# A two-layer convolution kernel: the prologue put in another order, the statistics' matrix product moved behind a group, small copies moved to ScalarE

## The chip, the cores and the metric

The kernel runs on 1 core of one Trainium2 chip. The metric is the device time of one execution in microseconds; lower is better. The engines are named as in the profile: PE (TensorE matmul), PEld (its weight loads), DVE (VectorE), ACT (ScalarE), POOL (GpSimd), SP (the queue that issues most DMAs).

## What is computed

Two layers, one after the other, on x of shape (8, 32, 252, 252), fp32. Each normalises its input over groups of two channels (16 groups, mean and variance over 2 x 252 x 252 values), convolves it with a 5 x 5 kernel over reflected padding (32 channels to 32), and adds the layer's input:

```python
def _gn(v, G=16, eps=1e-5):
    B_, C_, H_, W_ = v.shape
    g = v.reshape(B_, G, C_ // G, H_, W_)
    m = jnp.mean(g, axis=(2, 3, 4), keepdims=True)
    s = jnp.var(g, axis=(2, 3, 4), keepdims=True)
    return ((g - m) / jnp.sqrt(s + eps)).reshape(v.shape)

x = x + _L0_conv_ref(_gn(x), L0_conv_weight)   # _L0_conv_ref: reflect pad by 2, 5x5 convolution (written with fft2)
x = x + _L1_conv_ref(_gn(x), L1_conv_weight)
```

## The kernel before, in words

**Layout.** An image is split by parity of row and column into four quarter images (polyphase). The 128 partitions hold 4 parities x 32 channels; in each a padded quarter image has 128 x 128 points. A 5 x 5 convolution of the image becomes, on these 128 planes, a 3 x 3 convolution with 128 x 128 matrices. Along the rows it is done by a short transform (six products `m0` to `m5` give four output rows); along the columns by three accumulating matmuls with shifted views.

**Groups.** A *step* (b, l, T) is one group of 16 rows of image b in layer l. There are NG = 8 groups to an image and layer; a run of 8 is a *phase*. The phases are (0,0), (1,0), (0,1), (2,0), (1,1), ... , (7,1): 16 phases, 128 steps, 15 phase boundaries. Each step has six products of three fp32 matmuls, and the profile shows each matmul as two records, so 36 records.

**One step, in the order in which the code emits it.** Each engine works through its own instructions in that order (`manual_schedule`).
- `fetch` of step i+3 (SP: image rows into a buffer of two halves), chunk loads for the statistics (SP), `variance` in the step before a boundary.
- `transform` of step i+1 (DVE, L317 to L333): from the padded group `g` to the six inputs `v`.
- `scales` in the step before a boundary (DVE, L280 to L285: reciprocal standard deviation and `mr`).
- `conv` of step i: PE makes the products in the order m1, m2, m3, m4, m0, m5 (L359). ACT copies m1 (L374, adding the offset) and m3 (L382) out of PSUM, DVE combines (L378 to L396) into the output `y`. Between the products stand three hooks:
  - `after_1`: `prepare` of step i+2: layer 0 takes two ACT copies (L131) and three small POOL copies of the padding columns (L132, L134); layer 1 loads g from a DRAM scratch.
  - `after_3`: before a boundary `scale_matrices` (ACT, L292: the phase's matrices u = raw matrices x reciprocal deviation); for the group before, `to_output` (ACT copies L437, DMA) in layer 1 or `output_sums` (ACT, L251 and L252) in layer 0; `input_sums` of a chunk (ACT, L243 and L244).
  - `after_4`: `averages` two steps before a boundary, and `find_offset` and `add_own` one step before.
- At the end of a layer-0 `conv`, `to_scratch`: three small POOL copies of padding columns (L408 to L410) and the DMAs to the scratch (L418).

**Statistics.** Sums and sums of squares go by chunk into a slot tile. `averages` (L256 to L260) adds the slots on DVE (`tot`, L257) and multiplies them on PE with a membership matrix into PSUM (`pm`, L259). `variance` (L265 to L270) copies `pm` to SBUF (`me`) and takes the root on ACT; `scales` makes `mr`; `find_offset` (L304, L306) multiplies the matrix `total` with `mr` on PE (`po`) and copies it on DVE (`off`), which L374 adds; `add_own` (L300, DVE) adds the layer's own input to u. Of the three matmuls of a product, the first needs no result of `add_own`.

**Weights.** `load_taps` clears a tile on POOL (L143) and fills it with 8 DMAs on ACT's queue (L151). `make_matrices` takes sums (L162, L165) and makes six rows per tap on DVE (L171 to L180), clears u on POOL (L182) and copies the rows into it on ACT (L190, 8 copies). `make_own` makes a constant on POOL (L204, 24 operations).

**Prologue.** Taps of layer 0, rows of step 0, then the 8 chunks of image 0 through three buffers (a chunk's sum on DVE L241, its squares on ACT L244, in place, then the next load into that buffer), with the rest in between. The second layer's taps are loaded and turned into matrices behind step 1.

**Buffers.** Seven PSUM buffers for products, one for pm and po; two each for g, v and y.

Of the kernel before, what the change touches and what calls it, by code (L numbers as in the profile page):

```python
# [37 lines left out]
F32 = mybir.dt.float32  # L38
BF16 = mybir.dt.bfloat16
AF = mybir.ActivationFunctionType  # L40
ALU = mybir.AluOpType
AX = mybir.AxisListType

P = 128
# [12 lines left out]
def tile_conv_preact_x2(ctx: ExitStack, tc: tile.TileContext, x: bass.AP, w0: bass.AP, w1: bass.AP, out: bass.AP):  # L57
# [60 lines left out]
    def prepare(b: int, l: int, T: int):  # L118

        nr = min(GR + 2, PB - GR * T)  # L120
        g = gpool.tile([P, GR + 2, PB], F32, tag="g", name=f"g_{b}_{l}_{T}")
        gt[b, l, T] = g
        if nr < GR + 2:
            nc.gpsimd.memset(g[:, nr:, :], 0.0)  # L124
        if l:
            nc.sync.dma_start(g[:, :nr, :], scratch[b][:, GR * T : GR * T + nr, :])
            return
        t = xt.pop((b, T))
        h0, h1 = halves
        for pc in range(2):  # L130
            nc.scalar.copy(g[halves[pc], :nr, 1 - pc : 1 - pc + NB], t[:, :nr, 1 - pc : W : 2])  # L131
        nc.gpsimd.tensor_copy(g[h0, :nr, 0 : PB : PB - 1], g[h0, :nr, 1 : NB : NB - 2])  # L132
        for dst, src in ((126, 125), (127, 1)):
            nc.gpsimd.tensor_copy(g[h1, :nr, dst : dst + 1], g[h1, :nr, src : src + 1])  # L134


    ident = const.tile([P, P], F32, tag="ident", name="ident")
# [1 line left out]

    def load_taps(l: int, w: bass.AP):  # L140

        t = prep.tile([P, 2, 3, K, C], F32, tag="taps", name=f"taps{l}")
        nc.gpsimd.memset(t, 0.0)  # L143
        for pc in range(2):
            for pr in range(2):
                for rp in range(2):
                    d = pr - rp
                    rows = [a for a in range(3) if 0 <= 2 * a - d < K]
                    lo, n = rows[0], len(rows)
                    first = 2 * lo - d  # L150
                    nc.scalar.dma_start(  # L151
                        t[quad(pc, pr), rp, lo : lo + n], w[:, first : first + 2 * n - 1 : 2, :, :]
                    )
        return t

    def make_matrices(l: int, t: bass.AP):
        r = prep.tile([P, NF, 2, K, C], F32, tag="rows", name=f"rows{l}")
        s = prep.tile([P, 2, K, C], F32, tag="rsum", name=f"rsum{l}")
        v = nc.vector

        sums = prep.tile([P, C], F32, tag="sums", name=f"sums{l}")
        v.tensor_reduce(sums, t.rearrange("p r a k o -> p o (r a k)"), axis=AX.X, op=ALU.add)  # L162
        tot = const.tile([P, 4, C], F32, tag=f"total{l}", name=f"total{l}")
        for q in range(4):
            v.tensor_scalar(tot[:, q, :], sums, 0.25, None, ALU.mult)  # L165
        total.append(tot.rearrange("p q o -> p (q o)"))
        flat = lambda a: a.rearrange("p r k c -> p r (k c)")
        t0, t1, t2 = (flat(t[:, :, a]) for a in (2, 1, 0))
        s = flat(s)
        rf = [flat(r[:, f]) for f in range(NF)]  # L170
        v.tensor_scalar(rf[0], t0, 0.25, None, ALU.mult)  # L171
        v.tensor_copy(rf[5], t2)
        v.tensor_add(s, t0, t2)
        v.tensor_add(rf[1], s, t1)
        v.tensor_sub(rf[2], s, t1)
        v.tensor_scalar(r[:, 1:3].rearrange("p f r k c -> p (f r k c)"), r[:, 1:3].rearrange("p f r k c -> p (f r k c)"), -1.0 / 6, None, ALU.mult)
        v.scalar_tensor_tensor(s, t2, 4.0, t0, ALU.mult, ALU.add)
        v.scalar_tensor_tensor(rf[3], t1, 2.0, s, ALU.mult, ALU.add)
        v.scalar_tensor_tensor(rf[4], t1, -2.0, s, ALU.mult, ALU.add)
        v.tensor_scalar(r[:, 3:5].rearrange("p f r k c -> p (f r k c)"), r[:, 3:5].rearrange("p f r k c -> p (f r k c)"), 1.0 / 24, None, ALU.mult)  # L180
        u = const.tile([P, NF, 3, 2, 2, C], F32, tag=f"u{l}", name=f"u{l}")
        nc.gpsimd.memset(u, 0.0)  # L182
        for pc in range(2):
            for cp in range(2):
                d = pc - cp
                cols = [b for b in range(3) if 0 <= 2 * b - d < K]
                lo, n = cols[0], len(cols)
                first = 2 * lo - d
                for rp in range(2):
                    nc.scalar.copy(  # L190
                        u[halves[pc], :, lo : lo + n, 1 - cp, 1 - rp, :],
                        r[halves[pc], :, rp, first : first + 2 * n - 1 : 2, :],
                    )
        raw.append(u.rearrange("p f b c r o -> p (f b c r o)"))
# [17 lines left out]
    def make_averages():  # L212
        for l, pattern in enumerate(("p (q g e) -> p g q e", "p (g q e) -> p g q e")):
            kinds = {"q": 4, "e": 2}
            member = const.tile([P, C // 2], F32, tag=f"member{l}", name=f"member{l}")
            nc.vector.tensor_reduce(member, ident.rearrange(pattern, **kinds), axis=AX.XY, op=ALU.add)
            a = const.tile([P, 4, C // 2, 2], F32, tag=f"avg{l}", name=f"avg{l}")
            for q in range(4):
                for e in range(2):
                    nc.vector.tensor_scalar(a[:, q, :, e], member, 1.0 / COUNT, None, ALU.mult)  # L220
            avg.insert(0, a.rearrange("p q g e -> p (q g e)"))


# [22 lines left out]
    def output_sums(b: int, T: int, y: bass.AP):  # L246
# [4 lines left out]
        nc.scalar.activation(junk[:, :rows], view, AF.Identity, accum_out=st[:, 0, T : T + 1])  # L251
        nc.scalar.activation(junk[:, :rows], view, AF.Square, accum_out=st[:, 1, T : T + 1])  # L252

    def averages(b: int, l: int):

        tot = small.tile([P, 2], F32, tag="tot", name=f"tot_{b}_{l}")  # L256
        nc.vector.tensor_reduce(tot, sums.pop((b, l)), axis=AX.X, op=ALU.add)  # L257
        pm = ps_stat.tile([P, 2], F32, tag="pstat", name=f"pm_{b}_{l}")
        nc.tensor.matmul(pm, avg[l], tot, start=True, stop=True)  # L259
        norm[b, l] = pm  # L260

    def variance(b: int, l: int):
# [24 lines left out]

    ut, offset = {}, {}

    def scale_matrices(b: int, l: int):  # L290
        u = upool.tile([P, NF, 3, P], F32, tag="u", name=f"u_{b}_{l}")
        nc.scalar.activation(  # L292
            u.rearrange("p f b m -> p (f b m)"), raw[l], AF.Identity, scale=norm[b, l][:, 0:1]
        )
        ut[b, l] = u

    def add_own(b: int, l: int):
# [4 lines left out]
    def find_offset(b: int, l: int):  # L302
        po = ps_stat.tile([P, 1], F32, tag="pstat", name=f"po_{b}_{l}")
        nc.tensor.matmul(po, total[l], norm.pop((b, l))[:, 1:2], start=True, stop=True)  # L304
        offset[b, l] = small.tile([P, 1], F32, tag="off", name=f"off_{b}_{l}")
        nc.vector.tensor_copy(offset[b, l], po)  # L306


    vt = {}
# [37 lines left out]
    def conv(b: int, l: int, T: int, after_1, after_3, after_4):  # L347
# [46 lines left out]
        m5 = product(5)  # L394
        v.tensor_add(d1, m5, d1)  # L395
        v.scalar_tensor_tensor(yo[3], d2, 8.0, d1, ALU.mult, ALU.add)  # L396
        if l == 0:
            to_scratch(b, T, y)
        return y

    def to_scratch(b: int, T: int, y: bass.AP):
# [3 lines left out]
        yr = y[:, 0 : GR * PB].rearrange("p (r k) -> p r k", k=PB)  # L405
        h0, h1 = halves
        y1 = y[:, 1 : GR * PB + 1].rearrange("p (r k) -> p r k", k=PB)
        nc.gpsimd.tensor_copy(yr[h0, :rows, 0 : PB : PB - 1], yr[h0, :rows, 1 : NB : NB - 2])  # L408
        nc.gpsimd.tensor_copy(y1[h1, :rows, 126:127], y1[h1, :rows, 125:126])
        nc.gpsimd.tensor_copy(y1[h1, :rows, 127:128], y1[h1, :rows, 1:2])  # L410
        sc = scratch[b].rearrange("p r k -> p (r k)")
        for pc in range(2):
            for pr in range(2):
# [56 lines left out]
    one = const.tile([P, 1], F32, tag="one", name="one")  # L470
    nc.vector.memset(one, 1.0)
    nc.scalar.activation(one, one, AF.Sqrt)
    taps0 = load_taps(0, w0)
    fetch(*steps[0])
    chunks = {}
    BUFS = 3
    for c in range(BUFS):
        chunks[0, c] = input_chunk(0, c)
    make_identity(nc, ident)
    make_own()  # L480
    prepare(*steps[0])
    for c in range(NG):
        input_sums(0, c, chunks.pop((0, c)), early=True)
        if c + BUFS < NG:
            chunks[0, c + BUFS] = input_chunk(0, c + BUFS)
        if c == 1:
            make_averages()
        if c == 3:
            make_matrices(0, taps0)
        if c == 5:  # L490
            transform(*steps[0])
    averages(0, 0)
    variance(0, 0)
    scales(0, 0)
    scale_matrices(0, 0)
    find_offset(0, 0)
    add_own(0, 0)
    fetch(*steps[1])
    fetch(*steps[2])
    prepare(*steps[1])  # L500

    done = None
    for i, step in enumerate(steps):
# [3 lines left out]
            chunks[b, c] = input_chunk(b, c)  # L507
        for p in late.get(i, []):
            variance(*p)
        if i + 1 < N:  # L510
            transform(*steps[i + 1])
        for p in late.get(i, []):
# [6 lines left out]
        def after_3():  # L519
            for p in late.get(i, []):  # L520
                scale_matrices(*p)
            if done:
                (b, l, T), y = done
                if l:
                    to_output(b, T, y)
                else:
                    output_sums(b, T, y)
            for b, c in chunk_sum.get(i, []):
                input_sums(b, c, chunks.pop((b, c)))

        def after_4():
            for p in mid.get(i, []):
                averages(*p)
            for p in late.get(i, []):
                find_offset(*p)
                add_own(*p)

        done = step, conv(*step, after_1, after_3, after_4)
        if i == 1:
            make_matrices(1, load_taps(1, w1))  # L540
    to_output(*done[0][::2], done[1])


# [30 lines left out]
```

## Time and profile before

| | before |
|---|---|
| time, median of 3 runs | 2131.51 us (2128.77 to 2132.35) |
| profiled execution | 2128.59 us, its span 2126.5 us |
| mean granted PE clock | 0.978 |
| PE / DVE / ACT / POOL busy | 94% / 85% / 59% / 16% |
| PE's first group begins | 54.3 us |
| last PE matmul begins | 2115.7 us |

"Span" is from the first to the last instruction; the execution's own time is 2.1 us longer. In the timelines a row is: start, length, engine, line, operation, out<-in, count, and in brackets the idle time of the engine before it with what ended it. In the waits a row is: who waited for whom, us in total, times, the longest. In the groups: busy us, mean ns of one, idle before. Windows give for each stretch the busy time of the engines, then the granted PE clock, the DMA share and GB/s. Engines named with a q (SPq, ACTq) are the queues that issue DMAs.

### The profile page before, as it was taken

The page shows a single profiled execution, that of the slowest core. Times are in us where ns is not written, and L with a number is a line of the kernel's source. Part 1 is how long each engine was busy: PE and PEld are TensorE (multiplying, and loading weights), DVE is VectorE, ACT ScalarE, POOL GpSimd, SP SyncE. Part 2 cuts the span into 40 slices and gives each one's busy share as a digit, 9 for nine tenths or more (in the row PEclk, how much of TensorE's full clock was granted, in tenths as well). Part 3 has the DMA queues.
Part 4 walks back from the last instruction along what each step waited for, and adds up shares of the span by engine and source line. Part 5 has one row for each costly group of instructions (what it writes and reads, how often), then busy time and mean ns, then how long its engine had stood idle before and what let it go on. Part 6 is the DMA issues. An engine that isn't in the chain of part 4 may idle for free.

```text
span 2126.5 us, 15987 instructions
## 1 busy us (share of the span) xinstructions
PE 2001.9 (94%) x4672; PEld 891.7 (42%) x4672; DVE 1811.1 (85%) x2441; ACT 1248.7 (59%) x1186; POOL 341.4 (16%) x434
## 2 busy tenths in 40 slices
PE   0988999999999999999999999999999999999998
PEld 0433444444444444444444444444444444444443
DVE  6598889889798888889889899888979889799886
ACT  5687655666467664657555666566655666343333
POOL 2123320013200132002210023100321013200000
PEclk9989999999999999999999999999999999999999
DMA  7666757757567665775666666576756766445453
GB/s 225 192 159 134 157 141 225 202 123 157 169 212 178 134 136 161 230 188 122 142 198 208 144 143 154 193 210 139 154 145 217 198 132 142 116 136 144 123 155 85
DMA packets 179288, 346.80 MB, mean 163 GB/s; under 512 B 14080, under 2 KB 154624, under 8 KB 163840
## 3 DMA queue, kind: packets, MB, share of 16 engines
q1 hardware_dynamic: 177664, 344.95, 63.0%
q10 hardware_dynamic: 1536, 0.82, 0.2%
q8 instruction: 37, 0.61, 0.1%
q14 instruction: 51, 0.42, 0.1%
HBM read 213.58 MB, written 132.14 MB: 163 GB/s over the span
## 4 chain that ended last, share of the span: by engine, by line
PE 88%; DVE 6%; DMA 2%; ACT 2%; issue 1%; ACTq 0%; SPq 0%; POOL 0%; DVEq 0%; POOLq 0%
PE m L359 88%; DMA sx<-in_x_dram 1%; DVE ab L317 1%; DMA taps<-in_L_conv_weight_dram 1%; DVE y L388 0%; DVE y L389 0%; ACT sx L244 0%; DVE d L387 0%; ACT g L131 0%; DVE v L333 0%; DVE c L329 0%; PE pm L259 0%; DVE sums L241 0%; DVE s L386 0%; ACT o L437 0%
## 5 line engine op out<-in xcount | busy, mean ns | idle before, releaser
L359 PE MATMUL m<-v,u 128*128 128x504 f32 x4608 | 1991.7, 594 | 14.4 <-DVE v L326 13.0
L359 PEld LDWEIGHTS m<-v,u 128*128 128x128 f32 x4608 | 882.9, 192 | 1099.2 <-issue 1049.5
L374 ACT ACTIVATE a<-m,off 128x504 f32<-128x504 f32 x128 | 87.0, 680 | 368.7 <-PE m L359 368.6
L131 ACT COPY g<-x 64x2268 f32<-64x2268 f32 (+1 forms) x128 | 290.5, 2269 | 12.4 <-DMA x<-in_x_dram 10.1
L317 DVE SCALAR_TENSOR_TENSOR ab<-g 128x2048 f32<-128x2048 f32 x128 | 292.5, 2285 | 4.1 <-POOL g L134 3.8
L437 ACT COPY o<-y 64x1008 f32<-64x1008 f32 (+1 forms) x256 | 282.6, 1104 | 7.1 <-issue 4.0
L382 ACT COPY a<-m 128x504 f32<-128x504 f32 x128 | 74.2, 579 | 283.7 <-PE m L359 282.3
L408 POOL COPY y<-y 64x32 f32<-64x32 f32 x64 | 122.2, 1909 | 612.1 <-issue 336.7
L395 DVE TENSOR_TENSOR d<-m,d 128x504 f32<-128x504 f32 x128 | 87.3, 682 | 89.5 <-PE m L359 89.5
L392 DVE TENSOR_TENSOR s<-m,s 128x504 f32<-128x504 f32 x128 | 87.4, 683 | 89.2 <-PE m L359 78.1
L329 DVE TENSOR_TENSOR c<-g 128x1024 f32<-128x1024 f32 x128 | 156.4, 1222 | 0.0
L333 DVE TENSOR_TENSOR v<-ab 128x1024 f32<-128x1024 f32 x128 | 156.1, 1220 | 0.0
L386 DVE TENSOR_TENSOR s<-m,a 128x504 f32<-128x504 f32 x128 | 87.1, 681 | 53.2 <-PE m L359 37.7
L244 ACT ACTIVATE sx<-sx 128x2016 f32<-128x2016 f32 x64 | 118.8, 1857 | 10.4 <-issue 5.6
L252 ACT ACTIVATE junk<-y 128x2016 bf16<-128x2016 f32 x64 | 118.9, 1857 | 2.0
L251 ACT ACTIVATE junk<-y 128x2016 bf16<-128x2016 f32 x64 | 118.9, 1858 | 0.6
L132 POOL COPY g<-g 64x36 f32<-64x36 f32 x64 | 45.5, 712 | 445.4 <-ACT g L131 444.8
L243 ACT ACTIVATE sx<-sx 128x2016 f32<-128x2016 f32 (+1 forms) x56 | 103.6, 1850 | 4.7 <-DMA sx<-in_x_dram 4.0
L259 PE MATMUL pm<-tot,avg 128*128 128x2 f32 x32 | 8.0, 318 | 97.1 <-DVE tot L257 97.1
L124 POOL MEMSET g<- 128x256 f32 x16 | 5.0, 310 | 556.9 <-DVE c L329 556.4
L326 DVE TENSOR_TENSOR v<-ab 128x512 f32<-128x512 f32 x128 | 88.6, 692 | 4.4
L330 DVE SCALAR_TENSOR_TENSOR v<-c 128x512 f32<-128x512 f32 x128 | 88.6, 692 | 4.4
(61 smaller groups left out, 1148.9 us busy)
## 6 DMA issues: line engine op xcount, KB each, us to landing
g<-scratch SPq DMA_DIRECT2D x56, 1152.0 KB, 8.6
out_dram<-o SPq DMA_DIRECT2D x240, 252.0 KB, 3.7
x<-in_x_dram SPq DMA_DIRECT2D x104, 567.0 KB, 7.9
scratch<-y SPq DMA_DIRECT2D x224, 256.0 KB, 3.6
sx<-in_x_dram SPq DMA_DIRECT2D x56, 1008.0 KB, 7.2
g<-scratch SPq DMA_DIRECT2D x8, 1024.0 KB, 9.7
scratch<-y SPq DMA_DIRECT2D x32, 224.0 KB, 2.8
sx<-in_x_dram SPq DMA_DIRECT2D x8, 882.0 KB, 7.1
```

Source lines behind the costliest of these rows:

```text
L131: nc.scalar.copy(g[halves[pc], :nr, 1 - pc : 1 - pc + NB], t[:, :nr, 1 - pc : W : 2])
L243: nc.scalar.activation(t, t, AF.Identity, accum_out=st[:, 0, c : c + 1])
L244: nc.scalar.activation(t, t, AF.Square, accum_out=st[:, 1, c : c + 1])
L251: nc.scalar.activation(junk[:, :rows], view, AF.Identity, accum_out=st[:, 0, T : T + 1])
L252: nc.scalar.activation(junk[:, :rows], view, AF.Square, accum_out=st[:, 1, T : T + 1])
L317: v.scalar_tensor_tensor(flat, g[:, 0:GR, :].rearrange("p r k -> p (r k)"), -4.0, g[:, 2 : GR + 2, :].rearrange("p r k -> p (r k)"), ALU.mult,
L326: v.tensor_add(vs[0], ab[:, :, 2, :], ab[:, :, 1, :])
L329: v.tensor_sub(c.rearrange("p t r k -> p t (r k)"), rows_of(g, 3), rows_of(g, 1))
L333: v.tensor_sub(v05.rearrange("p t r k -> p t (r k)"), ab[:, :, 2:4, :].rearrange("p t r k -> p t (r k)"), ab[:, :, 0:2, :].rearrange("p t ...
L359: nc.tensor.matmul(ps, u[:, f, b3, :], vs[f][:, :, 2 - b3 : 2 - b3 + NB], start=(b3 == 0), stop=(b3 == 2),)
L408: nc.gpsimd.tensor_copy(yr[h0, :rows, 0 : PB : PB - 1], yr[h0, :rows, 1 : NB : NB - 2])
L437: nc.scalar.copy(o[halves[s], :n, 1 - pc : W : 2], yr[halves[pc], s * half : s * half + n, 1 : 1 + NB])
```

## The change

- Prologue: the three image chunks are loaded first, then step 0's rows, then the taps of both layers (two tiles, cleared on DVE). `make_averages` scales once on DVE and makes its copies on POOL. The six rows are made by `transform_taps` on POOL, in 12 operations without the fused ones; `sum_taps` (DVE) stands apart. Chunks 6 and 7 are summed on ACT, not DVE. `transform` of step 0 comes behind the chunks, the fetches of steps 1 and 2 ahead of the statistics. The first `scale_matrices` is on DVE, and `add_own` ahead of `find_offset`.
- The second layer's sums and rows are made ahead of step 0; its matrices are put together behind step 3.
- `averages` is split: `collect` (the sum on DVE) stands ahead of the step's `transform`, the product behind m5. `find_offset` too moves behind m5, and its copy of `off` to ACT.
- The padding copies in `prepare` and `to_scratch` move from POOL to ACT; `to_scratch` moves from the end of its step to `after_3` of the next.

```diff
--- before.py
+++ after.py
@@ -129,9 +129,9 @@
         h0, h1 = halves
         for pc in range(2):
             nc.scalar.copy(g[halves[pc], :nr, 1 - pc : 1 - pc + NB], t[:, :nr, 1 - pc : W : 2])
-        nc.gpsimd.tensor_copy(g[h0, :nr, 0 : PB : PB - 1], g[h0, :nr, 1 : NB : NB - 2])
+        nc.scalar.copy(g[h0, :nr, 0 : PB : PB - 1], g[h0, :nr, 1 : NB : NB - 2])
         for dst, src in ((126, 125), (127, 1)):
-            nc.gpsimd.tensor_copy(g[h1, :nr, dst : dst + 1], g[h1, :nr, src : src + 1])
+            nc.scalar.copy(g[h1, :nr, dst : dst + 1], g[h1, :nr, src : src + 1])
 
 
     ident = const.tile([P, P], F32, tag="ident", name="ident")
@@ -139,8 +139,8 @@
 
     def load_taps(l: int, w: bass.AP):
 
-        t = prep.tile([P, 2, 3, K, C], F32, tag="taps", name=f"taps{l}")
-        nc.gpsimd.memset(t, 0.0)
+        t = prep.tile([P, 2, 3, K, C], F32, tag=f"taps{l}", name=f"taps{l}")
+        nc.vector.memset(t, 0.0)
         for pc in range(2):
             for pr in range(2):
                 for rp in range(2):
@@ -153,31 +153,41 @@
                     )
         return t
 
-    def make_matrices(l: int, t: bass.AP):
+    def transform_taps(l: int, t: bass.AP):
+
         r = prep.tile([P, NF, 2, K, C], F32, tag="rows", name=f"rows{l}")
         s = prep.tile([P, 2, K, C], F32, tag="rsum", name=f"rsum{l}")
-        v = nc.vector
-
-        sums = prep.tile([P, C], F32, tag="sums", name=f"sums{l}")
-        v.tensor_reduce(sums, t.rearrange("p r a k o -> p o (r a k)"), axis=AX.X, op=ALU.add)
-        tot = const.tile([P, 4, C], F32, tag=f"total{l}", name=f"total{l}")
-        for q in range(4):
-            v.tensor_scalar(tot[:, q, :], sums, 0.25, None, ALU.mult)
-        total.append(tot.rearrange("p q o -> p (q o)"))
+        v = nc.gpsimd
         flat = lambda a: a.rearrange("p r k c -> p r (k c)")
         t0, t1, t2 = (flat(t[:, :, a]) for a in (2, 1, 0))
         s = flat(s)
         rf = [flat(r[:, f]) for f in range(NF)]
-        v.tensor_scalar(rf[0], t0, 0.25, None, ALU.mult)
-        v.tensor_copy(rf[5], t2)
+        both = lambda f: r[:, f : f + 2].rearrange("p f r k c -> p (f r k c)")
+
         v.tensor_add(s, t0, t2)
         v.tensor_add(rf[1], s, t1)
         v.tensor_sub(rf[2], s, t1)
-        v.tensor_scalar(r[:, 1:3].rearrange("p f r k c -> p (f r k c)"), r[:, 1:3].rearrange("p f r k c -> p (f r k c)"), -1.0 / 6, None, ALU.mult)
-        v.scalar_tensor_tensor(s, t2, 4.0, t0, ALU.mult, ALU.add)
-        v.scalar_tensor_tensor(rf[3], t1, 2.0, s, ALU.mult, ALU.add)
-        v.scalar_tensor_tensor(rf[4], t1, -2.0, s, ALU.mult, ALU.add)
-        v.tensor_scalar(r[:, 3:5].rearrange("p f r k c -> p (f r k c)"), r[:, 3:5].rearrange("p f r k c -> p (f r k c)"), 1.0 / 24, None, ALU.mult)
+        v.tensor_scalar(both(1), both(1), -1.0 / 6, None, ALU.mult)
+        v.tensor_scalar(rf[0], t2, 4.0, None, ALU.mult)
+        v.tensor_add(rf[0], rf[0], t0)
+        v.tensor_scalar(rf[5], t1, 2.0, None, ALU.mult)
+        v.tensor_add(rf[3], rf[0], rf[5])
+        v.tensor_sub(rf[4], rf[0], rf[5])
+        v.tensor_scalar(both(3), both(3), 1.0 / 24, None, ALU.mult)
+        v.tensor_scalar(rf[0], t0, 0.25, None, ALU.mult)
+        v.tensor_copy(rf[5], t2)
+        return r
+
+    def sum_taps(l: int, t: bass.AP):
+
+        sums = prep.tile([P, C], F32, tag="sums", name=f"sums{l}")
+        nc.vector.tensor_reduce(sums, t.rearrange("p r a k o -> p o (r a k)"), axis=AX.X, op=ALU.add)
+        tot = const.tile([P, 4, C], F32, tag=f"total{l}", name=f"total{l}")
+        for q in range(4):
+            nc.vector.tensor_scalar(tot[:, q, :], sums, 0.25, None, ALU.mult)
+        total.append(tot.rearrange("p q o -> p (q o)"))
+
+    def make_matrices(l: int, r: bass.AP):
         u = const.tile([P, NF, 3, 2, 2, C], F32, tag=f"u{l}", name=f"u{l}")
         nc.gpsimd.memset(u, 0.0)
         for pc in range(2):
@@ -214,10 +224,11 @@
             kinds = {"q": 4, "e": 2}
             member = const.tile([P, C // 2], F32, tag=f"member{l}", name=f"member{l}")
             nc.vector.tensor_reduce(member, ident.rearrange(pattern, **kinds), axis=AX.XY, op=ALU.add)
+            nc.vector.tensor_scalar(member, member, 1.0 / COUNT, None, ALU.mult)
             a = const.tile([P, 4, C // 2, 2], F32, tag=f"avg{l}", name=f"avg{l}")
             for q in range(4):
                 for e in range(2):
-                    nc.vector.tensor_scalar(a[:, q, :, e], member, 1.0 / COUNT, None, ALU.mult)
+                    nc.gpsimd.tensor_copy(a[:, q, :, e], member)
             avg.insert(0, a.rearrange("p q g e -> p (q g e)"))
 
 
@@ -251,12 +262,15 @@
         nc.scalar.activation(junk[:, :rows], view, AF.Identity, accum_out=st[:, 0, T : T + 1])
         nc.scalar.activation(junk[:, :rows], view, AF.Square, accum_out=st[:, 1, T : T + 1])
 
-    def averages(b: int, l: int):
-
+    def collect(b: int, l: int):
         tot = small.tile([P, 2], F32, tag="tot", name=f"tot_{b}_{l}")
         nc.vector.tensor_reduce(tot, sums.pop((b, l)), axis=AX.X, op=ALU.add)
+        norm[b, l] = tot
+
+    def averages(b: int, l: int):
+
         pm = ps_stat.tile([P, 2], F32, tag="pstat", name=f"pm_{b}_{l}")
-        nc.tensor.matmul(pm, avg[l], tot, start=True, stop=True)
+        nc.tensor.matmul(pm, avg[l], norm[b, l], start=True, stop=True)
         norm[b, l] = pm
 
     def variance(b: int, l: int):
@@ -287,11 +301,13 @@
 
     ut, offset = {}, {}
 
-    def scale_matrices(b: int, l: int):
+    def scale_matrices(b: int, l: int, first: bool = False):
         u = upool.tile([P, NF, 3, P], F32, tag="u", name=f"u_{b}_{l}")
-        nc.scalar.activation(
-            u.rearrange("p f b m -> p (f b m)"), raw[l], AF.Identity, scale=norm[b, l][:, 0:1]
-        )
+        flat, r = u.rearrange("p f b m -> p (f b m)"), norm[b, l][:, 0:1]
+        if first:
+            nc.vector.tensor_scalar(flat, raw[l], r, None, ALU.mult)
+        else:
+            nc.scalar.activation(flat, raw[l], AF.Identity, scale=r)
         ut[b, l] = u
 
     def add_own(b: int, l: int):
@@ -303,7 +319,7 @@
         po = ps_stat.tile([P, 1], F32, tag="pstat", name=f"po_{b}_{l}")
         nc.tensor.matmul(po, total[l], norm.pop((b, l))[:, 1:2], start=True, stop=True)
         offset[b, l] = small.tile([P, 1], F32, tag="off", name=f"off_{b}_{l}")
-        nc.vector.tensor_copy(offset[b, l], po)
+        nc.scalar.copy(offset[b, l], po)
 
 
     vt = {}
@@ -394,8 +410,6 @@
         m5 = product(5)
         v.tensor_add(d1, m5, d1)
         v.scalar_tensor_tensor(yo[3], d2, 8.0, d1, ALU.mult, ALU.add)
-        if l == 0:
-            to_scratch(b, T, y)
         return y
 
     def to_scratch(b: int, T: int, y: bass.AP):
@@ -405,9 +419,9 @@
         yr = y[:, 0 : GR * PB].rearrange("p (r k) -> p r k", k=PB)
         h0, h1 = halves
         y1 = y[:, 1 : GR * PB + 1].rearrange("p (r k) -> p r k", k=PB)
-        nc.gpsimd.tensor_copy(yr[h0, :rows, 0 : PB : PB - 1], yr[h0, :rows, 1 : NB : NB - 2])
-        nc.gpsimd.tensor_copy(y1[h1, :rows, 126:127], y1[h1, :rows, 125:126])
-        nc.gpsimd.tensor_copy(y1[h1, :rows, 127:128], y1[h1, :rows, 1:2])
+        nc.scalar.copy(yr[h0, :rows, 0 : PB : PB - 1], yr[h0, :rows, 1 : NB : NB - 2])
+        nc.scalar.copy(y1[h1, :rows, 126:127], y1[h1, :rows, 125:126])
+        nc.scalar.copy(y1[h1, :rows, 127:128], y1[h1, :rows, 1:2])
         sc = scratch[b].rearrange("p r k -> p (r k)")
         for pc in range(2):
             for pr in range(2):
@@ -470,33 +484,38 @@
     one = const.tile([P, 1], F32, tag="one", name="one")
     nc.vector.memset(one, 1.0)
     nc.scalar.activation(one, one, AF.Sqrt)
-    taps0 = load_taps(0, w0)
-    fetch(*steps[0])
+    BUFS = 3
     chunks = {}
-    BUFS = 3
     for c in range(BUFS):
         chunks[0, c] = input_chunk(0, c)
+    fetch(*steps[0])
+    taps = [load_taps(0, w0), load_taps(1, w1)]
     make_identity(nc, ident)
+    make_averages()
+    rows = transform_taps(0, taps[0])
     make_own()
-    prepare(*steps[0])
     for c in range(NG):
-        input_sums(0, c, chunks.pop((0, c)), early=True)
+        input_sums(0, c, chunks.pop((0, c)), early=c < 6)
         if c + BUFS < NG:
             chunks[0, c + BUFS] = input_chunk(0, c + BUFS)
         if c == 1:
-            make_averages()
+            sum_taps(0, taps[0])
         if c == 3:
-            make_matrices(0, taps0)
-        if c == 5:
-            transform(*steps[0])
+            prepare(*steps[0])
+        if c == 4:
+            make_matrices(0, rows)
+    transform(*steps[0])
+    fetch(*steps[1])
+    fetch(*steps[2])
+    collect(0, 0)
     averages(0, 0)
     variance(0, 0)
     scales(0, 0)
-    scale_matrices(0, 0)
+    scale_matrices(0, 0, first=True)
+    add_own(0, 0)
     find_offset(0, 0)
-    add_own(0, 0)
-    fetch(*steps[1])
-    fetch(*steps[2])
+    sum_taps(1, taps[1])
+    rows = transform_taps(1, taps[1])
     prepare(*steps[1])
 
     done = None
@@ -507,6 +526,8 @@
             chunks[b, c] = input_chunk(b, c)
         for p in late.get(i, []):
             variance(*p)
+        for p in mid.get(i, []):
+            collect(*p)
         if i + 1 < N:
             transform(*steps[i + 1])
         for p in late.get(i, []):
@@ -524,20 +545,22 @@
                 if l:
                     to_output(b, T, y)
                 else:
+                    to_scratch(b, T, y)
                     output_sums(b, T, y)
             for b, c in chunk_sum.get(i, []):
                 input_sums(b, c, chunks.pop((b, c)))
 
         def after_4():
-            for p in mid.get(i, []):
-                averages(*p)
             for p in late.get(i, []):
-                find_offset(*p)
                 add_own(*p)
 
         done = step, conv(*step, after_1, after_3, after_4)
-        if i == 1:
-            make_matrices(1, load_taps(1, w1))
+        for p in mid.get(i, []):
+            averages(*p)
+        for p in late.get(i, []):
+            find_offset(*p)
+        if i == 3:
+            make_matrices(1, rows)
     to_output(*done[0][::2], done[1])
 
 
```

## The prediction

> **What bounds the kernel now.** I read the page first, then the waits of PE, PE's timeline, and the timelines of DVE and ACT around one phase boundary and over the prologue.
>
> ```profile
> PE 2001.9 (94%) x4672; PEld 891.7 (42%) x4672; DVE 1811.1 (85%) x2441; ACT 1248.7 (59%) x1186; POOL 341.4 (16%) x434
> ...
> PE 88%; DVE 6%; DMA 2%; ACT 2%; issue 1%; ACTq 0%; SPq 0%; POOL 0%; DVEq 0%; POOLq 0%
> ```
>
> PE bounds it, so only time in which PE waits, or runs at a lower clock, can be saved. The waits of PE, then its timeline (start, length, group, idle before it):
>
> ```profile
> PE pm L259 <- DVE tot L257: 97.1, 16, 49.6
> PE m L359 <- DVE v L326: 13.0, 1, 13.0
> ...
> 54.32 48.90 PE L359 MATMUL m<-v,u 128*128 128x504 f32 x108 [1.47 <-ACT u L292]
> 116.18 58.83 PE L359 MATMUL m<-v,u 128*128 128x504 f32 x132 [12.96 <-DVE v L326]
> 181.25 0.59 PE L259 MATMUL pm<-tot,avg 128*128 128x2 f32 x2 [6.25 <-DVE tot L257]
> 181.70 17.93 PE L359 MATMUL m<-v,u 128*128 128x504 f32 x36
> ...
> 199.89 106.72 PE L359 MATMUL m<-v,u 128*128 128x504 f32 x252
> ...
> 436.91 0.38 PE L259 MATMUL pm<-tot,avg 128*128 128x2 f32 x2 [2.94 <-DVE tot L257]
> ```
>
> A full-speed stretch is 252 records in 106.72 us, 0.4235 each; a group has 36, so 15.25 us. PE waits in four places: 54.3 us of prologue; 12.96 us at 103 us; 6.25 us at the first phase boundary; and 97.1 - 49.6 - 6.25 = 41.25 us over the 14 later ones (2.94 each). The 36 records behind those 14 boundaries, by windows with the granted clock in the column after PEld (three kinds, and the sum):
>
> ```profile
> 437.16:452.64 15.48, 15.45 (x36) 6.70 (x36) 1.00 0.56 118
> ...
> 691.65:708.83 17.18, 17.15 (x36) 7.32 (x36) 0.90 0.50 106
> ...
> 1075.28:1093.65 18.37, 18.28 (x36) 7.79 (x36) 0.85 0.50 150
> ...
> sum 245.86, PE 245.05 PEld 104.79; mean PE 17.50 PEld 7.48
> ```
>
> One of the 14 stays at clock 1.00 and takes 15.45; the others run at 0.84 to 0.91. So the waits also cost clock: 245.05 - 14 x 15.45 = 28.75 us. [...]
>
> **The change at a boundary.** Today the sum `tot` (L257) stands behind four DVE operations that need m4, and PE waits there, between m4 and m0. Rows of DVE at one boundary, with two of ACT:
>
> ```profile
> 434.07 0.68 DVE L386 TENSOR_TENSOR s<-m,a 128x504 f32<-128x504 f32 x1 [0.50 <-PE m L359]
> ...
> 436.70 0.16 DVE L257 TENSOR_REDUCE tot<-sums 128x2 f32<-128x16 f32 x1
> ...
> 443.23 0.68 DVE L396 SCALAR_TENSOR_TENSOR y<-d,d 128x504 f32<-128x504 f32 x1
> ...
> 444.34 2.28 DVE L317 SCALAR_TENSOR_TENSOR ab<-g 128x2048 f32<-128x2048 f32 x1
> ...
> 452.43 0.16 DVE L285 SCALAR_TENSOR_TENSOR mr<-me,mr 128x1 f32<-128x1 f32 x1
> 452.51 0.68 DVE L378 TENSOR_TENSOR s<-m,a 128x504 f32<-128x504 f32 x1
> ...
> 456.37 1.13 DVE L300 TENSOR_TENSOR u<-u,own 64x384 f32<-64x384 f32 x2
> ...
> 424.66 0.19 ACT L244 ACTIVATION_READ_ACCUMULATOR sx<-sx 128x1 f32 x1
> ...
> 452.43 2.22 ACT L292 ACTIVATE u<-u,mr 128x2304 f32<-128x2304 f32 x1 [1.43 <-DVE mr L284]
> ```
>
> Now `collect` stands ahead of the transform and the product behind m5. I count from t = 0, the start of m1 in the group before the last (423.80: m4 ends at 436.91 - 2.94 = 433.97, four products or 24 x 0.4235 = 10.16 us on). The last sums are in at 424.85, before DVE is done with the group before (t = 1.4), so `collect` waits for nothing and costs DVE 0.2. m5 ends at 15.25, pm takes 0.25 and the last group begins at 15.5. L396 starts 0.8 behind m5's end, at 16.0; from there as in the rows: ab at 17.1 (1.1 on), mr at 25.2, L378 at 25.3 (8.17 behind ab). Without the moved `off` copy, add_own follows L389 directly and runs 29.1 to 30.2; ACT scaled u at 25.2 to 27.4. PE ends m5 at 30.75, does po (mr 5 us old), and needs own 0.85 us later, at 31.8. Margin 1.6 us: no wait. What is late next is add_own, and only past that margin. Behind PE's two products nothing waits that is on the path: DVE reads pm after two operations that need m5 anyway; ACT's `off` copy (0.2, as its smallest rows) is queued behind the output copies and wanted by a1, 9 us before DVE needs that. Saved: 41.25 + 28.75 = 70.0 us.
>
> **Padding copies on ACT, `to_scratch` later.** Three small copies per layer-0 `prepare` and three per `to_scratch`; ACT's floor and the same copies on POOL:
>
> ```profile
> L270 ACT ACTIVATE std<-var 128x1 f32<-128x1 f32 x16 | 3.2, 203 | 134.8 <-DVE var L268 134.8
> ...
> L408 POOL COPY y<-y 64x32 f32<-64x32 f32 x64 | 122.2, 1909 | 612.1 <-issue 336.7 <-DVE y L396 178.6 <-ACT sx L243 83.2
> L134 POOL COPY g<-g 64x18 f32<-64x18 f32 (+1 forms) x128 | 64.4, 533 | 100.3 <-ACT g L131 99.3 <-DMA scratch<-y 1.0
> ...
> 228.35 0.58 ACT L382 COPY a<-m 128x504 f32<-128x504 f32 x1
> ...
> 232.76 0.19 ACT L252 ACTIVATION_READ_ACCUMULATOR junk<-y 128x1 f32 x1
> 238.20 0.68 ACT L374 ACTIVATE a<-m,off 128x504 f32<-128x504 f32 x1 [5.26 <-PE m L359]
> ```
>
> At 0.2 each, 1.2 us per layer-0 group, against 5.26 us that ACT idles in it: nothing on the path. a3 moves from 8.5 to 9.1 us after the group's start, DVE wants it at 10.2. SP issues the scratch writes some 8 us later, behind the next fetch instead of ahead; their reader is a phase away, and y's buffer is wanted 11 us into the group after. Without that cover they would cost 1.2 x 64 = 77 us. The ends are 0.2 and POOL's 0.5 to 1.9; I take the floor, because ACT's rows show a fixed part of 0.2 and (2.22 - 0.20) / 2304 = 0.88 ns an element, so 0.03 for 36.
>
> **Phase 0 and the second layer's matrices.** The 12.96 us were DVE waiting for the second taps and then making rows; loads and rows now lie in the prologue, and ACT alone makes u copies (4.15 us) after group 3. With that go 2.9 us of low clock (132 records in 58.83 instead of 55.9), and the first boundary's 6.25 + 2.5 (17.93 instead of 15.45). Before: 24.6 us. But here ACT is full: per group
>
> ```profile
> L131 ACT COPY g<-x 64x2268 f32<-64x2268 f32 (+1 forms) x14 | 31.5, 2251 | 0.3
> L251 ACT ACTIVATE junk<-y 128x2016 bf16<-128x2016 f32 x6 | 11.3, 1886 | 0.1
> ...
> L190 ACT COPY u<-rows 64x576 f32<-64x576 f32 (+1 forms) x8 | 4.1, 587 | 18.2 <-DVE rows L180 18.2
> ...
> 69.76 1.88 ACT L243 ACTIVATE sx<-sx 128x2016 f32<-128x2016 f32 x1 [3.96 <-DMA sx<-in_x_dram]
> ```
>
> two g copies 4.6 (the mean holds a shorter form), a1 and a3 1.25, output sums 3.9 with their reads, chunk sums of the same shape 3.9, pads 1.2: 14.9 of 15.25. Group 0 has three chunks, whose loads land at T0 + 15.4 today (T0 is PE's first group, 54.3) and at 14.7 then, as `prepare` no longer stands behind ACT's scaling; so ACT leaves it at T0 + 26.4, and 4.15 come on top after group 3. Going on at 14.9 a group, the last chunk sum ends at T0 + 104.6, group 6 starting at 94.5 on PE (the first group is 3 longer at the low clock: 108 records in 48.90). PE does not wait up to there: transforms and seven PSUM buffers run one group ahead. `collect` then holds DVE until 104.8, DVE ends group 6 at 118.6, mr is at 127.6 and own at 132.2, while PE ends group 7 at 125.3 and has 1.1 to do before own: it waits 5.8 us; clock as behind the 13 us gap, 2.9. After: 8.7. Saved: 15.9 us. Bounds: no stall (24.6 saved) to twice it (7).
>
> **Prologue.** Rows of before:
>
> ```profile
> L204 POOL TENSOR_SCALAR own<-ident 32x64 f32<-32x64 f32 x24 | 8.6, 361 | 1.4
> L182 POOL MEMSET u<- 128x2304 f32 x2 | 4.0, 2020 | 0.1
> ...
> SPq L115 <- DMA taps<-in_L_conv_weight_dram: 4.9, 1, 4.9
> ...
> sx<-in_x_dram SPq DMA_DIRECT2D x56, 1008.0 KB, 7.2
> ...
> 27.71 0.32 DVE L171 TENSOR_SCALAR rows<-taps 128x320 f32<-128x320 f32 x1
> ...
> 31.49 0.49 DVE L180 TENSOR_SCALAR rows<-rows 128x640 f32<-128x640 f32 x1
> ...
> 47.57 1.67 ACT L244 ACTIVATE sx<-sx 128x1764 f32<-128x1764 f32 x1
> ```
>
> The end is set by ACT: last sum read at 49.35, PE starts 4.95 later. Scaling on DVE (640 elements 0.49, so 2304 about 1.4) instead of ACT's 2.2 takes 0.8 off. POOL makes 12 row operations: the floor is DVE's ten in 4.3 us, the ceiling own's 361 ns for 64 elements scaled up (320: 1.8, 640: 3.6), 25 us; I take 9, a fixed 0.3 and memset's 0.88 ns an element, twice for two inputs. [...]
> Sixteen tap loads now stand at the head of ACT's queue, and issues on both queues wait for earlier landings (4.9 us above). If the taps go first, ACT is free at about 9.5 us; chunks 1 and 2, held up behind taps to 10, land 7.2 and one chunk later, at 17 and 19, and chunk 3 behind them; from 24 on ACT is full: squares 4.1, g 5.1, u 4.15, three chunks' last 9.8: last sum 46.8, T0 51. If the chunk and image loads go first, the last tap waits for the image (13.5), ACT is free at 18, POOL has taps at 17, then rows 9, own 10, memset 2: 38, and ACT's u copies stand behind that: last sum 50 to 53, T0 54 to 57. I put T0 at 54.3, no change; the bounds stand in the range. The second taps' 2.2 us of sums on DVE lie where it waits for g, the tap memsets (0.9 on POOL today) and POOL's 16 copies of the averages where both engines wait for the first loads; without that cover they would cost 2.2, 1.8 and 2.7 (0.17 each).
>
> **Sum.** 70.0 + 15.9 = 85.9; the profiled execution took 2128.6, so 2042.7. It lies 2.9 below the median of the runs shown (2131.5, from 2128.8 to 2132.4); I forecast 2044. The runs differ by 0.17%, so 0.2% is about what can be told from no change.
>
> **Rivals.** (1) own is late at every boundary by 1 us, 2.6 us more than counted, and half a clock step comes back (1.7): 15 x 2.7 = 40, 2084. For it: DVE has only 1.4 us of slack a group; against: the 1.6 us margin. Chance 0.15. (2) POOL at its ceiling: taps 17, rows 25, own 10, memset 2: 54, and ACT still has 4.15 + 9.8 behind it, so T0 72, 18 us more: 2061. For it: POOL's y copy takes 0.23 alone and 1.9 on average beside DVE. Chance 0.10. (3) Slower: the six copies make ACT the bound of layer-0 groups. Today's work there is 10 of 15.25; over 5.3 us (0.88 a copy) each group stretches, and from 6.6 (1.1 a copy, 64 groups x 1.34 = 86) the kernel is slower; at 1.2 a copy 2043 + 64 x 1.9 = 2165. For it: POOL's y copy at 1.9 and g copies at 0.5 each; against: ACT's 0.2 row, and that the largest of the six has 36 elements a partition. Chance 0.03. (4) The product waits as long in its new place, since `collect` waits for sums: then only phase 0 gains, 2113. Against: sums in at 424.85. Chance 0.04.
>
> **Numbers.** My forecast 0.68, 2031 (T0 51, no stall at the first boundary) to 2053. With (2) and part of (1) the range is 2029 to 2068. Faster: all but (3) and a bit, 0.95; same 0.02; slower 0.03.
>
> **What would show it.** Right: pm and po without idle before them; clock 1.00 in the 36 records behind 14 boundaries; no 13 us gap near 100; one stall of 4 to 8 us at the first boundary; ACT's pad copies near 0.2. Wrong: idle of PE's m behind add_own or u at each boundary, a first group later than 58 us, or ACT without idle in layer-0 groups.

## The result, and the profile after

| | before | after |
|---|---|---|
| time, median | 2131.19 us (2128.77 to 2132.35, 4 runs) | 2030.12 us (2029.06 to 2031.15, 4 runs) |
| profiled execution / its span | 2128.59 / 2126.5 us | 2029.54 / 2027.8 us |
| mean granted PE clock | 0.978 | 0.997 |

The ratio is 0.9527, 95% interval 0.9511 to 0.9544: 4.7% faster. Forecast were 2044 us and a range of 2029 to 2068; the time lies 14 us below the forecast, 1 us inside the range's low edge and just below the 2031 to 2053 that had a chance of 0.68.

The busy row of the page after, and its chain: PE's share of the span rises from 94% to 97%, POOL falls from 341 us to 48, ACT rises from 1249 to 1331 (the padding copies).

```profile
PE 1960.0 (97%) x4672; PEld 879.9 (43%) x4672; DVE 1799.5 (89%) x2392; ACT 1331.0 (66%) x1589; POOL 48.5 (2%) x88
...
PE 90%; ACT 4%; DVE 2%; DMA 2%; issue 1%; SPq 0%; ACTq 0%; DVEq 0%
```

The waits of PE (who waited for whom, us in total, times, longest):

```profile
PE pm L273 <- DVE tot L267: 50.6, 1, 50.6
PE po L320 <- DVE mr L299: 4.4, 2, 2.2
PE m L375 <- ACT u L310: 1.5, 1, 1.5
```

And PE's timeline (start, length, operation, number of records, and in brackets the idle time ahead and what ended it), over the first boundaries and the last:

```profile
54.96 108.64 PE L375 MATMUL m<-v,u 128*128 128x504 f32 x252 [0.98 <-DVE u L308]
163.43 0.28 PE L273 MATMUL pm<-tot,avg 128*128 128x2 f32 x2
163.57 15.46 PE L375 MATMUL m<-v,u 128*128 128x504 f32 x36
181.20 0.58 PE L320 MATMUL po<-mr,total 128*128 128x1 f32 x2 [2.17 <-DVE mr L299]
183.25 2.05 PE L375 MATMUL m<-v,u 128*128 128x504 f32 x2 [1.47 <-ACT u L310]
185.46 107.14 PE L375 MATMUL m<-v,u 128*128 128x504 f32 x250 [0.16 <-DVE u L316]
292.44 0.28 PE L273 MATMUL pm<-tot,avg 128*128 128x2 f32 x2
292.58 15.46 PE L375 MATMUL m<-v,u 128*128 128x504 f32 x36
...
1880.09 0.28 PE L273 MATMUL pm<-tot,avg 128*128 128x2 f32 x2
```

Of the wait of 97.1 us in 16 pieces one piece is left, the prologue's. The 13 us gap near 100 us is gone. Behind every boundary but the first, 36 records take 15.46 us, and PE runs on; windows over two such stretches have the clock at 1.00:

```profile
292.58:307.88 15.30, 15.30 (x40) 6.89 (x39) 14.76 (x27) 8.13 (x12) 0.00 (x0) 1.00 0.47 154
1758.10:1773.39 15.29, 15.29 (x39) 6.89 (x38) 14.75 (x27) 6.70 (x10) 0.00 (x0) 1.00 0.31 86
```

From the second boundary's pm to the last boundary's there are 13 phases: (1971.58 - 309.55) / 13 = 127.85 us before, (1880.09 - 292.44) / 13 = 122.13 after. So a boundary gave 5.72, and 14 of them 80.1. The prologue ends 0.6 us later (54.96 against 54.32). The rest of the 98.7 us of span, some 19, came from phase 0 and the first boundary.

### The profile page after: what moved, and what is told of

Its sections match the earlier page's. It is cut to its first block, busy times and chain, and to the rows that moved or that the text cites. A ratio compares the mean times of both kernels' runs of the same rounds, so it can differ in the third digit from the quotient of the medians.

```text
span 2027.8 us, 15748 instructions
## 1 busy us (share of the span) xinstructions
PE 1960.0 (97%) x4672; PEld 879.9 (43%) x4672; DVE 1799.5 (89%) x2392; ACT 1331.0 (66%) x1589; POOL 48.5 (2%) x88
## 4 chain that ended last, share of the span: by engine, by line
PE 90%; ACT 4%; DVE 2%; DMA 2%; issue 1%; SPq 0%; ACTq 0%; DVEq 0%
PE m L375 90%; ACT g L131 1%; DMA sx<-in_x_dram 1%; DMA taps<-in_L_conv_weight_dram 1%; ACT sx L255 1%; ACT sx L254 1%; DVE ab L333 0%; ACT u L200 0%; ACT o L451 0%; ACT junk L262 0%; ACT junk L263 0%; DVE y L404 0%; DVE y L405 0%; DVE v L342 0%; DVE d L403 0%
## 5 line engine op out<-in xcount | busy, mean ns | idle before, releaser
L375 PE MATMUL m<-v,u 128*128 128x504 f32 x4608 | 1958.2, 587 | 2.6 <-ACT u L310 1.5
L375 PEld LDWEIGHTS m<-v,u 128*128 128x128 f32 x4608 | 869.8, 189 | 1067.4 <-issue 1014.8
L408 DVE TENSOR_TENSOR s<-m,s 128x504 f32<-128x504 f32 x128 | 87.4, 683 | 12.6 <-DVE y L405 0.5
L404 DVE SCALAR_TENSOR_TENSOR y<-d,d 128x504 f32<-128x504 f32 x128 | 87.4, 683 | 12.1 <-ACT o L451 8.0
L405 DVE SCALAR_TENSOR_TENSOR y<-s,s 128x504 f32<-128x504 f32 x128 | 87.4, 683 | 4.4
L409 DVE TENSOR_TENSOR y<-s,s 128x504 f32<-128x504 f32 x128 | 87.4, 683 | 4.4
L412 DVE SCALAR_TENSOR_TENSOR y<-d,d 128x504 f32<-128x504 f32 x128 | 87.4, 683 | 4.4
```

The source lines that it names most:

```text
L375: nc.tensor.matmul(ps, u[:, f, b3, :], vs[f][:, :, 2 - b3 : 2 - b3 + NB], start=(b3 == 0), stop=(b3 == 2),)
```

## Experiments

Each kernel was timed beside the kernel before. Times are medians, and two changed kernels are best compared by their ratios to before. The first four, and e8, ask which part of the change brought the 5.72 us, and why.

**e1: the kernel before with the boundary part alone.**

```diff
 step i:
+    collect (mid steps)            # the sum on DVE, ahead of transform
     transform(i + 1)
     m1 m2 m3 m4
-    averages / find_offset         # PE, between m4 and m0
     m0 m5
+    averages / find_offset         # PE, behind m5; off copied on ACT
```

> The kernel before, with the boundary part alone: the sum ahead of the transform, both products behind m5, the offset copied on ACT. Theory (the boundary work carries most of the gain): about 80 us go at the 14 later boundaries (idle 3.1 with PE's drain, clock 2.0, slower small products 0.3 to 0.6 each), some 5 more at the first; the 13 us gap near 103 us stays. 2040 to 2048. Rival (the gain comes from the copies that left GpSimd, or the parts need each other): above 2070.

2041.52 us, ratio 0.9582 (0.9569 to 0.9595). The boundary part carries 89 of the 101 us. Its PE waits show the 13 us gap as it was, and none for DVE's sum but the prologue's:

```profile
PE m L362 <- DVE v L329: 12.8, 1, 12.8
```

**e2 and e3: each half of the boundary part taken back from the changed kernel.**

```diff
 e2                                      e3
+ after_4: averages                     - ahead of transform: collect
- behind m5: averages                   + after_4: collect
```

> The changed kernel with the averaging product back between m4 and m0, the sum still ahead of the transform. Theory (PE waited for DVE's sum, not for its own place in the order): no idle at pm, 2030 within 2 us. Rival (the place behind the group is what helps): PE waits again, 2060 to 2110.

> The changed kernel with the sum back behind four DVE operations that need m4, the product still behind m5. Theory: DVE has the sum 2.95 us behind m4, PE has 5.1 us of m0 and m5 to do before the product, so no idle either: 2030 within 2 us; at the first boundary perhaps 1 to 3 us better, as the transform no longer stands behind the last chunk sum there. Rival (the sum must be early): idle at pm, above 2050.

e2: 2029.67 us, ratio 0.9525 (0.9512 to 0.9538). e3: 2028.95 us, ratio 0.9521 (0.9508 to 0.9534). Neither can be told from the whole change (0.9527). One of the two is enough: with the sum early, PE finds it in either place of the product; with the product late, PE does m0 and m5 while DVE catches up. One boundary of each, e2 first, shows the product without idle before it:

```profile
776.22 0.28 PE L273 MATMUL pm<-tot,avg 128*128 128x2 f32 x2
776.36 20.53 PE L375 MATMUL m<-v,u 128*128 128x504 f32 x48
```

```profile
781.38 0.28 PE L273 MATMUL pm<-tot,avg 128*128 128x2 f32 x2
781.51 15.46 PE L375 MATMUL m<-v,u 128*128 128x504 f32 x36
```

In e3 only the first boundary keeps a wait of the product (4.15 us) in place of the ones for po and u. The 1 to 3 us that were expected there did not come: from PE's first group to the second pm it takes 238.4 us, against 237.5 in the changed kernel.

**e4: both halves taken back.** `collect` and `averages` both in `after_4`; everything else as changed.

> The changed kernel with sum and product both back in the old place (the offset product stays behind m5). Theory: 2.94 us of idle and the lower clock come back at 14 boundaries, 5.4 to 5.7 us each, and a wait of some 6 us at the first in place of the 6.9 lost there now: 2103 to 2112. [...] Rival (product place matters little now that copies left GpSimd): under 2060.

2108.98 us, ratio 0.9898 (0.9884 to 0.9911), 79 us above the changed kernel. The wait returns to within 0.01 us, and with it the slow stretch: behind the 14 later boundaries 48 records take 21.93 to 23.58 us, 22.57 on average, where e2 has 20.53. One of them:

```profile
1059.66 0.59 PE L273 MATMUL pm<-tot,avg 128*128 128x2 f32 x2 [2.94 <-DVE tot L267]
1060.11 23.33 PE L375 MATMUL m<-v,u 128*128 128x504 f32 x48
```

**e8: how much of the price is clock.** The sum stands behind two of the four operations that need m4, so PE idles for less; the product stands between m4 and m0.

```diff
         v.tensor_sub(d2, a3, m4)
+        collect (mid steps)
         v.scalar_tensor_tensor(yo[1], d2, 2.0, d1, ALU.mult, ALU.add)
```

> The changed kernel with the sum behind two DVE operations that need m4 (not four) and the product between m4 and m0: PE idles about 1.6 us at each of 15 boundaries instead of 2.94. What a short wait costs in clock: nothing, 2030 + 15 x 1.8 (idle, drain) = 2057; as much as after 2.94 us (2.0 each), 2087; in some boundaries, between them.

2057.04 us, ratio 0.9654 (0.9638 to 0.967). At the 14 later boundaries PE idles 1.51 us and the clock does not fall:

```profile
291.24 0.38 PE L273 MATMUL pm<-tot,avg 128*128 128x2 f32 x2 [1.51 <-DVE tot L267]
291.48 20.53 PE L375 MATMUL m<-v,u 128*128 128x504 f32 x48
```

The window over that stretch of e8, with the granted clock behind the engines' columns:

```profile
291.24:312.00 20.76, 20.76 (x53) 9.57 (x53) 17.32 (x31) 11.54 (x16) 0.00 (x0) 1.00 0.49 156
```

From pm to pm a phase is 123.90 us here ((1778.09 - 291.24) / 12), 1.77 above the changed kernel; in e4 it is 127.54 ((1952.61 - 294.56) / 13), 5.41 above. An idle of 1.51 us costs 1.77; one of 2.94 costs 5.41. The 1.43 us between them cost 3.64, and of the surplus of 2.2 the slower records, 22.57 against 20.53, are 2.0: that is the clock.

**e5: the padding copies back on GpSimd.** The five `nc.scalar.copy` lines of `prepare` and `to_scratch` are `nc.gpsimd.tensor_copy` again; `to_scratch` stays in the next step.

> The changed kernel with all padding copies back on GpSimd (the scratch writes stay in the next group). Theory: the copies on ACT bought nothing, and cost where ACT is full, in phase 0: 1.2 us a group less there, so the last chunk sum comes some 6 us earlier, and the 6.9 us lost at the first boundary shrink to 0 to 3: 2023 to 2026. Rival (GpSimd copies hold up DVE or the scratch writes): 2030 or slower.

2023.07 us, ratio 0.9494 (0.948 to 0.9508). This part of the change costs 7 us. What e5 has and e1 has not (the new prologue, the second layer's matrices ahead of step 0, `to_scratch` later) brings some 18 us by the two ratios; no run takes these apart. On ACT the copies take what was forecast (rows of the changed kernel):

```profile
L132 ACT COPY g<-g 64x36 f32<-64x36 f32 x64 | 16.5, 258 | 1.6
L422 ACT COPY y<-y 64x32 f32<-64x32 f32 x64 | 15.8, 247 | 1.0
```

but in phase 0 ACT is full (busy for 103.6 of the 108.5 us from PE's first group to the next pm), and the last chunk's sum, for which DVE's `tot` of the first boundary waits, comes 5.9 us later. That row in the changed kernel and in e5:

```profile
158.58 0.17 DVE L267 TENSOR_REDUCE tot<-sums 128x2 f32<-128x16 f32 x1 [2.58 <-ACT sx L255]
```

```profile
152.69 0.17 DVE L267 TENSOR_REDUCE tot<-sums 128x2 f32<-128x16 f32 x1 [1.70 <-ACT sx L255]
```

From the first pm to the second it is 129.01 us in the changed kernel (6.88 above 122.13) and 123.00 in e5 (285.59 - 162.59; 0.87 above). Besides these 6.0 us, e5's PE starts 0.67 us earlier.

**e6 and e7: the second taps off ACT's queue, alone and with e5.**

```diff
-    taps = [load_taps(0, w0), load_taps(1, w1)]
+    taps = [load_taps(0, w0, nc.scalar)]
 ...
     fetch(*steps[2])
+    taps.append(load_taps(1, w1, nc.sync))
```

> The changed kernel with the second layer's eight tap loads issued on SP behind the fetches of steps 1 and 2, not at the head of ACT's queue. Theory (ACT, which had its first chunk at 5.6 us and began at 15.1, was held by those issues): ACT begins near 8, SP too issues chunk 2 and the image earlier, PE's first group starts at 46 to 50 instead of 55.0: 2021 to 2026. Rival (the prologue is bound by the chunk loads or by GpSimd's rows): 2028 to 2030.

> Both of the two edits (padding copies on GpSimd, second taps on SP). If they act in different places, the gains add: 2015 to 2020.

Both expectations failed. e6: 2032.85 us, ratio 0.9538 (0.9523 to 0.9552); e7: 2025.80 us, ratio 0.9507 (0.9493 to 0.9521): no faster than without the edit. In e6 ACT does begin earlier, 9.68 us against 15.14 (the first two rows, changed kernel and then e6), but loses the lead in three places. Chunk 3's load is not earlier by as much: ACT takes it at 25.57, against 27.95. Then ACT waits for GpSimd to clear u, behind the rows and `own`; and GpSimd's rows of the second taps now run beside the short DVE chain that leads to PE's start.

```profile
15.14 1.88 ACT L255 ACTIVATE sx<-sx 128x2016 f32<-128x2016 f32 x1 [12.91 <-DMA taps<-in_L_conv_weight_dram]
```

```profile
9.68 1.88 ACT L255 ACTIVATE sx<-sx 128x2016 f32<-128x2016 f32 x1 [7.45 <-DMA taps<-in_L_conv_weight_dram]
...
38.56 4.14 ACT L200 COPY u<-rows 64x576 f32<-64x576 f32 x8 [4.03 <-POOL u L192]
...
55.25 0.85 POOL L169 TENSOR_TENSOR rows<-rsum,taps 128x320 f32<-128x320 f32 x1
55.34 0.78 DVE L299 SCALAR_TENSOR_TENSOR mr<-me,mr 128x1 f32<-128x1 f32 x1
```

The last operation ahead of u's scaling takes 0.78 us there, 0.16 in the changed kernel; PE's first group starts at 57.50.

**e9 and e10: built on that.** e9 is e5 with both u tiles cleared on GpSimd ahead of the rows, the second taps on SP behind chunk 5, their sums behind group 1; e10 puts the first taps on SP too.

```diff
+    clear = [clear_matrices(0), clear_matrices(1)]      # GpSimd, while it waits for taps
     rows = transform_taps(0, taps[0])
 ...
+        if c == 2:
+            taps.append(load_taps(1, w1, nc.sync))
 e10:
-    taps = [load_taps(0, w0, nc.scalar)]
+    taps = [load_taps(0, w0, nc.sync)]                  # sum_taps(0) behind chunk 5
```

> Padding copies on GpSimd as in e5; the second taps on SP behind chunk 5's load; both u tiles cleared on GpSimd ahead of the rows, while it waits for taps; the second taps' sums behind group 1. Theory (e6 freed ACT 5.5 us earlier, and lost it waiting 4.0 us for u to be cleared and about 1 us to GpSimd's rows beside the short DVE chain): with u cleared early PE starts at 49 to 52, 2018 to 2021, against 2023 for e5. Rival (chunk loads bind): no better than e5.

> e9 with the first taps too on SP, behind the image rows, and their sums on DVE behind chunk 5: nothing but the table load stands ahead of ACT's squares. Theory (the tap issues on ACT, and chunk 2 waiting for a tap's landing, hold the start): ACT begins at 8, PE at 45 to 48: 2013 to 2017. Rival (GpSimd's rows, which get their taps some 3 us later, bind): PE at 50 or later, 2018 to 2023.

e9: 2021.43 us, ratio 0.9490 (0.9477 to 0.9503), PE's first group at 51.50. It is the fastest of the kernels run, though its interval overlaps e5's, so the rival (no better than e5) is not excluded. PE starts 2.8 us earlier than in e5, but up to the second boundary's pm 1.8 of them are lost; where was not traced. e10: 2028.25 us, ratio 0.9526 (0.9513 to 0.9539). Its ACT begins at 8.05 and still has its last chunk at 46.47, against 47.10 in e9: chunk 3, whose load SP issues behind the taps, keeps ACT idle for 9.3 us. Its transform then waits 10.3 us for padding copies that stand behind `own` in GpSimd's queue, and PE starts at 57.95. Neither of its two expected ranges holds; the rival had the mechanism (GpSimd's rows come late), but the taps reach GpSimd 8 us later than in e9 (19.16 against 10.93), not 3.

```profile
24.74 1.88 ACT L258 ACTIVATE sx<-sx 128x2016 f32<-128x2016 f32 x1 [9.31 <-DVE sums L255]
...
42.53 2.29 DVE L336 SCALAR_TENSOR_TENSOR ab<-g 128x2048 f32<-128x2048 f32 x1 [10.26 <-POOL g L134]
```

## Why the prediction was right, point by point

- **The boundary: right in kind, short by 10 us.** Forecast were 70.0 us for 14 boundaries, measured 80.1 (5.72 each, not 5.00). The term was mis-sized because only idle time and the slower 36 records were counted. The idle of 2.94 is counted from the modelled end of the last record, 0.585 us long, while records follow each other at 0.423 (252 of them in the 106.56 us from 308.01 to the next pm at 414.57); so each wait loses 0.16 more. And pm and po themselves got shorter: from pm's start to the next product 0.44 or 0.25 before (1074.84 to 1075.28; 436.91 to 437.16), 0.14 after; behind po 0.24 before, 0.14 after, and 0.18 in front of it. That is 0.16 + 0.2 + 0.1 + 0.2 and accounts for nearly all of the 0.72. e8 bears it out: 1.51, 0.16 and 0.10 for its pm (0.24 against 0.14) make its 1.77. e2 and e3 show more than the prediction claimed: either move would have done.
- **The 1.6 us margin of add_own** held: no wait for it at any later boundary. Rival 1 (late own everywhere, 2084) is out, rival 4 (the wait stays, 2113) too.
- **The clock** came back as forecast (28.75 us by the rows). e4 and e8 put the point between 1.51 us of idle (no fall at any of the 14 boundaries: 48 records in 20.53) and 2.94 (slower records at all 14). In the kernel before, the granted clock is 0.50 or 0.51 already over pm at seven of the 14 boundaries (309.55 to 310.00 is one) and 1.00 at the others, so at those seven the clock had fallen by the end of the 2.94 us wait. In e4 it is 0.87 over the records behind the first of its 2.94 us waits (295.00 to 318.58).
- **Phase 0 and the first boundary: the mechanism as forecast, the size 3 to 4 us short.** `collect` was to be held until T0 + 104.8 and mr to come at T0 + 127.6; measured are 158.58 and 181.15, T0 + 103.6 and 126.2. PE then idles 3.8 us in three pieces (2.17 for mr, 1.47 for u, 0.16 for own), not 5.8 for own alone; the boundary costs 6.88, not 8.7, and the first group's slow clock 1.9 us, not 3.
- **The padding copies** were costed at nothing, with ACT's idle time as cover. That holds in later phases: e5's later phases are no shorter (from the second pm to the end of the span 1735.3 us, against 1735.4). In phase 0 the same text counts them in ACT's 14.9 of 15.25 us, and there e5 shows that they cost 6 to 7 us. So the forecast's 8.7 us held their cost, but the text did not name it as theirs: nearly all of that stall was the price of this one part of the change. Rival 3 (ACT becomes the bound, 2165) would have needed 0.88 us a copy; they take 0.21 to 0.26.
- **The prologue** was put at no change between 51 and 57: it is 54.96. That it came so near is partly luck, as neither of its two cases happened: ACT began at 15.1, between 9.5 and 18, and GpSimd's rows took 12.6 us (10.90 to 23.53), not 9, but got their taps at 10.9, not 17, so that u was clear at 35.6, before ACT came to it at 36.8. The 9 was an estimate from a fixed 0.3 and 0.88 ns an element, twice for two inputs; before has no two-input operation on GpSimd that shows the doubling (on DVE, 320 elements with two inputs took 0.48 and 640 with one 0.49). In the changed kernel a two-input operation on 320 elements took 0.86, as the estimate has it, but a multiplication with one input 1.01 on 320 and 1.81 on 640, where it has 0.58 and 0.86. Rival 2 (GpSimd at its ceiling) did not come about, but e6 shows the same mechanism once ACT is earlier.

For the profiled execution 2042.7 us were forecast and 2029.5 measured. Of these 13 us, 10 were the boundary term and 3 to 4 phase 0 with the first boundary; the prologue took 0.6 back.

## What to carry to other kernels

A product on the critical engine that needs a result of another engine may be moved behind work that is ready, or its operand may be made earlier; either is enough, and the rows say how much cover is wanted (here 2.95 us against 5.1 of two products). Price a wait of PE by the last record's tail and by the clock that it loses, not by its idle time alone: here 2.94 us cost 5.4 to 5.7, and 1.51 cost 1.77. Work moved to an engine that is idle on average is to be priced in the stage where that engine is full, and work moved out of a queue helps only if the next queue in line is free.

## What the runs showed of the hardware that was not expected

On GpSimd a one-input multiplication was slower than a two-input addition of the same size (1.01 against 0.86 us for 320 elements, and 1.81 for 640):

```profile
12.66 0.85 POOL L169 TENSOR_TENSOR rows<-rsum,taps 128x320 f32<-128x320 f32 x1
13.60 1.81 POOL L170 TENSOR_SCALAR rows<-rows 128x640 f32<-128x640 f32 x1
15.47 1.01 POOL L171 TENSOR_SCALAR rows<-taps 128x320 f32<-128x320 f32 x1
```

And GpSimd and DVE were slower beside each other in both directions: GpSimd's two-input operation of 0.86 us took 2.27 beside DVE's transform (35.66 us in the changed kernel), while in e6 a DVE operation on one element per partition took 0.78 instead of 0.16 beside GpSimd's rows (55.34 us, while a two-input operation of 0.85 ran from 55.25). In e9 the same DVE operation took 0.16 while GpSimd was in a one-input multiplication (from 48.43, 1.81 long). What makes the two slower was not tested.
